# A second Strassen step for pairs of text units, and half of the adapter's turns on VectorE

## The chip, the cores and the metric

One core of a Trainium2 chip runs the whole program. The metric is the time of one execution in microseconds on the device (us below). TensorE (PE in the profile; its weight loads are PEld), VectorE (DVE), ScalarE (ACT), GpSimd (POOL) and SyncE (SP, which here only issues DMAs) each work through their own list of instructions in order, and wait for each other by semaphores.

## What is computed

The reference is a cross attention with an adapter path, all in float32. `x` is 2 batches of 2048 rows of 640 columns, `ctx` 2 batches of 128 tokens of 384 columns; the last 4 tokens are the adapter's.

```python
residual = x
enc, ca = ctx[:, :124], ctx[:, 124:]
query, keyt, valt = x @ Wq, enc @ Wk, enc @ Wv
hs = _mha(query, keyt, valt)                       # 8 heads of 80
ca_q1 = einsum('btc,th->bch', ca, Wq_ca)[:, indices, :]   # 2048 rows, indices = linspace(0, 383, 2048)
ca_hs1 = _mha(ca_q1, residual, residual)
ca_hs2 = _mha(ca_hs1 @ Wq, ca @ Wk_ca, ca @ Wv_ca)
out = (hs + ca_hs2) @ Wout + b_out + residual
```

Since `ca_q1` holds only 384 different rows for each batch, the adapter path is worked out for these 384, and its result (`o2`) is added to the output rows by an index at the end.

## The kernel before

**How the order is set.** Every operation of the program is issued by a `Desk` (line 66). Pieces of work are generators that yield `Do(engine, function, what it waits for, rooms it needs)`; `Desk.run` (line 351) issues them in the order of a table of whole numbers, `TURNS` (line 85 on), one number for each operation: the number divided by 6 is the place in the order, the remainder names the engine. So the table sets the program order of each engine and, where an operation may run on either of two engines, which one takes it. On the chip each engine keeps its program order and waits for semaphores alone; the table's numbers are no times.

**TensorE's helpers.** `matmul` (L396) is a plain product. `by_columns` (L405) splits a product with 128 output rows over the four column groups of 32 of the array, which work at the same time. A float32 product takes two passes, so a product of 128x128 by 128xN through `by_columns` is four rows in the order and 8 MATMUL records of width N in the trace. I call these 8 a **set** of width N. `transpose` (L410) turns a 128x128 block by a product with the identity (a turn, below). VectorE, ScalarE and GpSimd operations all pass through `call` (L427), DMAs through `dma` (L447).

**Stages.** At the start, weights and the first rows are loaded and turned, and small combined weights (`pk`, `pa`, `pyz`, `pv`) are made; VectorE spreads turned pieces and copies, and turns the rows of `x` with its own transposes (`xi` to `xt`, four instructions of 128x512 and one of 128x4x128 for each block of 512 rows). Then 8 blocks of queries follow (`pq`), mixed with the adapter's first pass over the scores (`s`, maxima `mx` by VectorE), and the text scores (`sc`, `softmax`), whose probabilities go to HBM and come back turned (`kept`, `pT`).

**The adapter** (`adapter(b)`, line 1869, for batch b = 0, 1): after the maxima, `spread` leaves them in `mt`, two halves j of 128x384 (j = 0, 1). For each half TensorE turns three blocks of 128x128 (`pm`), VectorE adds them to `ca`, and both halves are split into `cop` together. Then comes the second pass over the scores with `cop`, in 12 pieces for each half, whose exponentials are contracted with the values (`contract`, line 1985, tile `acc`). At the end of each half TensorE turns three blocks of `accs` into `pt_acc`, and after both halves `second(b)` (line 2030) makes `o2`.

**The text units.** 16 units m of 256 rows (two tiles of 128 rows each) go through `probabilities(m)` (line 2242) and `text_out_fast(m)` (line 2392). This takes the heads' outputs `ph` into `hs` (four chunks of 128 and a fifth that is apart), makes the sums s1 to s4 of a Strassen step (on VectorE or GpSimd), and takes (256 rows x 512) by (512 x 640) in seven products of half size rather than eight: 7 products of two chunks each, and four products for the fifth chunk, so 18 sets of width 320 (`HALF`). They stand in four chains of 4, 2, 1 and 1 steps (`chains`); a chain accumulates in one PSUM bank `po`, and after each step VectorE adds what the bank holds by then into a quarter (128 rows x 320 columns) of the residual rows (`add` in `chain`). A step waits for the add of the step before it in its chain. The residual rows lie in two times four row slots (`x_more`, `last_rows`), a tile each; when a tile has its sums, `stored` lets GpSimd add `o2` by an indirect DMA (L2351) and sends it out. The last unit had `o2` added earlier, and its halves of 320 columns go out one by one (`stored_half`).

## Time and profile before

| what | value |
|---|---|
| time, median of 3 runs | 573.14 us (573.0 to 573.99) |
| the profiled execution, its own time | 573.35 us |
| its span in the profile | 571.3 us |
| granted TensorE clock | 1.00 throughout |
| busy share of the span | PE 99%, PEld 54%, DVE 69%, ACT 50%, POOL 28% |
| MATMUL records | 8069 |

The span runs from the first to the last record of the profiled execution. The time of the same execution is 2.05 us longer, and it stands 0.21 us above the median. Times in rows are in us unless ns is said; a row of groups gives busy time and the mean of one instruction, then the idle time of the engine ahead of it; a row of a timeline gives its start and its length, and joins instructions of one kind that follow each other.

### The profile page before, as it was taken

How to read it: one execution, taken by the hardware profiler on the slowest of the kernel's cores; microseconds unless marked ns; L12 is line 12 of the kernel's file. 1: busy time of each engine (PE TensorE's matmuls, PEld its weight loads, DVE VectorE, ACT ScalarE, POOL GpSimd, SP SyncE). 2: the span in 40 equal slices, each digit the busy share in tenths (PEclk: the TensorE clock that was granted, in tenths of full speed). 3: DMA queues.
4: the chain of work that ended last, by engine and by line, in shares of the span. 5: the costliest groups of instructions: out<-in, count | busy, mean ns of one | idle time of the engine just before them, and what ended most of it. 6: DMA issues, size and time to landing. Idle time of an engine off the chain costs nothing.

```text
span 571.3 us, 18875 instructions
## 1 busy us (share of the span) xinstructions
PE 563.6 (99%) x8069; PEld 310.0 (54%) x8069; DVE 394.4 (69%) x659; ACT 286.7 (50%) x806; POOL 159.8 (28%) x213
## 2 busy tenths in 40 slices
PE   9999999999999999999999999999999999999997
PEld 8885335455555455466554554554555554445553
DVE  4366999999998577458999999998332213544443
ACT  2021355645566899899876654524554664100000
POOL 9102041114440731100004350531203053045152
PEclk9999999999999999999999999999999999999999
DMA  8998576965968977446746969977476587799888
GB/s 246 211 248 126 139 161 157 172 179 139 211 212 153 215 182 211 146 126 198 233 158 203 316 180 319 245 217 230 96 263 120 164 206 223 248 211 213 258 156 237
DMA packets 145691, 113.21 MB, mean 198 GB/s; under 512 B 82548, under 2 KB 116980, under 8 KB 145608
## 3 DMA queue, kind: packets, MB, share of 16 engines
q1 hardware_dynamic: 137000, 95.10, 60.0%
q0 software_dynamic: 5632, 10.69, 11.7%
q10 hardware_dynamic: 2976, 6.23, 3.2%
q8 instruction: 63, 1.03, 0.8%
q14 instruction: 20, 0.16, 0.1%
HBM read 71.60 MB, written 40.39 MB: 196 GB/s over the span
## 4 chain that ended last, share of the span: by engine, by line
PE 92%; DVE 3%; ACT 3%; DMA 1%; issue 1%; SPq 0%; ACTq 0%; DVEq 0%
PE po L405 27%; PE pq L405 24%; PE sc L396 7%; PE acc L396 7%; PE s L396 7%; PE ph L396 6%; PE pq L396 4%; PE pyz L396 2%; ACT ea L427 2%; DVE mx L427 2%; PE pv L396 1%; PE pk L396 1%; DMA xz<-in_x_dram 1%; ACT p L427 1%; PE pt_wq L410 1%
## 5 line engine op out<-in xcount | busy, mean ns | idle before, releaser
L427 ACT ACTIVATE p<-sc,m 128x124 f32<-128x124 f32 x256 | 90.1, 381 | 43.4 <-DVE m L427 38.4
L427 DVE TENSOR_REDUCE mx<-s 128x4 f32<-128x2048 f32 x48 | 109.0, 2271 | 1.9 <-PE s L396 1.9
L427 ACT ACTIVATE ea<-s 128x2048 f32<-128x2048 f32 x48 | 90.5, 1884 | 31.4 <-PE s L396 30.9
L405 PE MATMUL po<-wout_sums,hs 128*32 128x320 f32 x1024 | 78.5, 434 | 0.1
L405 PE MATMUL po<-wout_sb,hs 128*32 128x320 f32 x928 | 72.4, 433 | 0.0
L427 POOL TENSOR_TENSOR p<-p,r 128x992 f32<-128x992 f32 x17 | 31.4, 1847 | 130.9 <-DVE r L427 130.9
L405 PE MATMUL pq<-xt,wq_sb 128*32 128x256 f32 (+1 forms) x928 | 66.4, 418 | 0.0
L427 DVE TENSOR_TENSOR last_rows<-last_rows,po 128x320 f32<-128x320 f32 x60 | 28.1, 480 | 44.0 <-PE po L405 43.9
L427 ACT ACTIVATION_READ_ACCUMULATOR p<-sc,m 128x1 f32 x256 | 57.0, 223 | 0.0
L427 DVE TENSOR_TENSOR x_more<-x_more,po 128x320 f32<-128x320 f32 x68 | 32.4, 481 | 34.5 <-PE po L405 32.5
L405 PEld LDWEIGHTS po<-wout_sums,hs 128*32 128x32 f32 x1024 | 33.4, 110 | 32.7 <-issue 2.8
L427 DVE TENSOR_REDUCE m<-sc 128x4 f32<-128x496 f32 x64 | 40.8, 663 | 14.1 <-PE sc L396 14.0
L396 PE MATMUL acc<-ea,y_sb 128*32 128x384 f32 (+2 forms) x768 | 50.2, 382 | 0.2 <-ACT ea L427 0.2
L396 PE MATMUL ph<-pT,vpad 128*32 128x256 f32 x768 | 47.9, 381 | 0.0
L405 PEld LDWEIGHTS po<-wout_sb,hs 128*32 128x32 f32 x928 | 30.1, 110 | 28.2 <-issue 1.6
L2351 POOL DMA_INDIRECT x_more<-o,query x17 | 26.6, 1563 | 67.0 <-DVE x_more L427 31.1
L405 PEld LDWEIGHTS pq<-xt,wq_sb 128*32 128x32 f32 x928 | 27.7, 110 | 28.0 <-issue 13.4
L427 ACT COPY hs<-ph 128x512 f32<-128x512 f32 (+1 forms) x25 | 13.4, 551 | 57.7 <-PE ph L396 57.7
L427 DVE STREAM_TRANSPOSE eb<-p 128x1024 f32<-128x1024 f32 x32 | 39.4, 1233 | 1.2 <-POOL p L427 1.1
L396 PEld LDWEIGHTS sc<-kmain,q 64*128 64x128 f32 x512 | 31.8, 187 | 12.6 <-issue 5.8
L427 POOL TENSOR_TENSOR hs<-hs 128x256 f32<-128x256 f32 x31 | 28.9, 1019 | 33.9 <-ACT hs L427 25.6
L396 PE MATMUL sc<-kmain,q 64*128 64x124 f32 x512 | 38.0, 285 | 0.0
(219 smaller groups left out, 835.0 us busy)
## 6 DMA issues: line engine op xcount, KB each, us to landing
kept<-eb SPq DMA_DIRECT2D x32, 512.0 KB
pT<-kept SPq DMA_DIRECT2D x16, 1024.0 KB
landing<-away SPq DMA_DIRECT2D x15, 512.0 KB
xi<-in_x_dram SPq DMA_DIRECT2D x56, 128.0 KB
x_more<-in_x_dram SPq DMA_DIRECT2D x17, 320.0 KB
last_rows<-in_x_dram SPq DMA_DIRECT2D x15, 320.0 KB
y<-yt SPq DMA_DIRECT2D x16, 256.0 KB
y_sb<-y SPq DMA_DIRECT2D x32, 128.0 KB
```

Of the source, the lines that this page charges most:

```text
L396: self.pin(self.nc.tensor.matmul(out, lhsT, rhs, **kw))
L405: self.pin(self.nc.tensor.matmul(out[j : j + 32], lhsT[:, j : j + 32], rhs, **kw))
L410: self.pin(self.nc.tensor.transpose(out, in_, ident))
L427: self.pin(getattr(engine, what)(*args, **kw))
L2351: desk.pin(nc.gpsimd.indirect_dma_start(out=t, out_offset=None, in_=o2_of[b], in_offset=bass.IndirectOffsetOnAxis(ap=query[:, st : st + 1] ...
```

## The change

**Text units.** Ten of the 16 units are joined in five pairs, `PAIRED = ((6, 7), (3, 12), (9, 14), (10, 11), (8, 15))`. Three of the seven products of a unit's Strassen step (p = 0, 1, 2) are no longer taken for each unit apart: `joint` takes each for the two units of a pair at once, by a second Strassen step inside (two units x two chunks by two chunks x two halves of 160 columns), seven products of 128x160 rather than eight. `take_inner` makes the weights' inner differences once (`inner_w`, and two freed tiles `p_0`, `p_1`; 12 subtractions), `joint` the inner sums of `hs` for each pair (`inner_x`, 8 operations). The products stand in chains of 4, 2, 1 and 1 steps of width 160 (`inner_chain`, tiles `pi_n_p_c`), and each step is added by VectorE to an eighth (128 x 160) of the residual rows. Of a paired unit's own chains there remain the first and a step that is added to two quarters. The units' order is now 0, 4, 2, 1, 5, 13 and then the pairs; `probabilities` of a paired unit waits until the unit before has its room. The last unit's step of one product is split in two parts of 160 columns, and its first tile goes out in quarters.

**The adapter.** Only half j = 0 of the maxima is turned by TensorE. Half j = 1 is turned by VectorE in 16 transposes of 32x3x32 (`turned_blocks`), in a piece of work of its own (`other_half`), and the second pass of j = 0 waits for its own half of `cop` only. Of the four `pt_acc`, that of batch 1, half 0, is turned by VectorE too.

**The start.** `load_ca` waits for the masks only, the clearing of `vpad` for `ctx`, and all of `TURNS` holds new numbers. In the program lists, SP's load of `w_k` now stands behind all four loads of `xi` of the second block, where it stood ahead of them.

**Counts in the order, before and after:** sets of width 320 in the text units 288 and 196; sets of width 160 there 0 and 169; turns for `pm` 12 and 6, for `pt_acc` 12 and 9; VectorE adds of 128x320 into the rows 128 and 106, of 128x160 0 and 124; inner sums of `hs` 0 and 40 (20 on VectorE, 20 on GpSimd), inner differences of the weights 0 and 12 (5 and 7); VectorE transposes of 32x3x32 0 and 48; sums of `x` on VectorE 7 and 2, on GpSimd 17 and 22.

In the lists below line numbers of after are its own: L425, L434, L439 and L456 are `matmul`, `by_columns`, `transpose` and `call`, which were L396, L405, L410 and L427.

TensorE towards the end of the adapter's second pass of batch 1, where units of the text stand between its pieces (`po_n` is chain n of a unit, `wout_sums` holds sums of the weights and also the fifth chunk of `hs`; x4 and x8 are one and two sets). Before, a piece in which two units' chains alternate:

```order
L405 MATMUL po_0_6335<-wout_sums,hs_5064 32x320 x8
L405 MATMUL po_2_6537<-wout_sb,hs_5064 32x320 x8
L405 MATMUL po_2_6537<-wout_sb,wout_sums 32x320 x4
L405 MATMUL po_2_6554<-wout_sb,hs_4229 32x320 x8
L405 MATMUL po_2_6554<-wout_sb,wout_sums 32x320 x4
L405 MATMUL po_0_6568<-wout_sb,hs_4229 32x320 x8
L405 MATMUL po_1_6398<-wout_sums,hs_5064 32x320 x8
L405 MATMUL po_1_6398<-wout_sb,wout_sums 32x320 x4
L405 MATMUL po_0_6335<-wout_sb,wout_sums 32x320 x4
L405 MATMUL po_0_6568<-wout_sums,hs_4229 32x320 x8
```

And after, the same stretch of the program (`pi_0_0_6444` is the chain of four steps of product p = 0 of one pair; `p_834` and `p_835` hold inner differences of the weights):

```order
L434 MATMUL pi_0_0_6444<-wout_sb,hs_4137 32x160 x4
L434 MATMUL pi_2_0_6349<-wout_sb,wout_sums 32x160 x4
L434 MATMUL pi_1_0_6458<-wout_sb,hs_4137 32x160 x4
L434 MATMUL pi_0_0_6444<-p_834,inner_x_5623 32x160 x4
L425 MATMUL acc_1_5909<-ea_1_10_6387,y_sb 32x256 x8
L434 MATMUL pi_0_0_6444<-p_834,inner_x_5623 32x160 x4
L425 MATMUL acc_1_5909<-ea_1_11_6441,y_sb 32x128 x4
L425 MATMUL acc_1_5909<-ea_1_11_6441,y_sb 32x384 x4
L434 MATMUL pi_0_0_6444<-wout_sb,wout_sums 32x160 x4
L434 MATMUL pi_1_0_6458<-p_835,inner_x_5624 32x160 x4
```

Steps of a chain of width 160 now stand between those of others: the first two of `pi_0_0_6444` have two sets of width 160 between them, where the two steps of `po_0_6568` before have four sets of width 320.

VectorE at the start, before (`k_160` from the loaded `w_k`, `k_414` from TensorE's `p_kca`, then the first transpose of the second block's rows):

```order
L427 COPY k_160<-w_k 128x3x4x16 x2
L427 COPY k_414<-p_kca 128x128
L427 COPY k_414<-p_kca 128x16 x2
L427 TENSOR_TENSOR wide<-k_414,quarter 128x128
L427 TENSOR_REDUCE own<-ident 128x4
L427 TENSOR_SCALAR own<-own,side_83 128x4 x2
L427 TENSOR_REDUCE fold<-ident 128x32
L427 STREAM_TRANSPOSE xt_1_395<-xi_1_275 128x512
```

And after, from the copy out of `p_kca` on (now `k_420`):

```order
L456 COPY k_420<-p_kca 128x128
L456 COPY k_420<-p_kca 128x16 x2
L456 STREAM_TRANSPOSE xt_1_378<-xi_1_285 128x512
L456 TENSOR_TENSOR wide<-k_420,quarter 128x128
L456 TENSOR_REDUCE own<-ident 128x4
L456 TENSOR_SCALAR own<-own,side_83 128x4 x2
L456 TENSOR_REDUCE fold<-ident 128x32
L456 STREAM_TRANSPOSE xt_1_378<-xi_1_285 128x512 x3
L456 COPY k_160<-w_k 128x3x4x16 x2
L456 STREAM_TRANSPOSE xt_1_378<-xi_1_285 128x4x128
```

The two copies of `w_k` into `k_160` have moved from ahead of the copy out of `p_kca` to behind four transposes of `xt_1`. On TensorE the product that reads them (`pk_482`) stands here after, with the first rows that follow:

```order
L439 MATMUL pt_k_467<-ident,k_420 128x128
L425 MATMUL pt_k_467<-fold,wide 128x6
L425 MATMUL unread<-zeros 128x128
L439 MATMUL pt_wqca<-ident,wqca_sb 128x4 x2
L439 MATMUL pt_wqca<-ident,wqca_rest 128x4 x3
L425 MATMUL pk_482<-ctxT,k_160 128x256 x3
L425 MATMUL pa_0_494<-first_rows,blk_k 32x128 x16
```

Before, that product (`pk_457`) stood three rows behind `p_kca`; it is now the last ahead of `pa`.

TensorE between the adapter's two passes of batch 1 (`pm` turns the maxima), before:

```order
L405 MATMUL po_0_5181<-wout_sums,hs_5064 32x320 x8
L410 MATMUL pm_0_5227<-ident,mt_5190 128x128 x3
L410 MATMUL pm_1_5234<-ident,mt_5190 128x128 x3
L405 MATMUL po_0_5197<-wout_sums,hs_4130 32x320 x8
L405 MATMUL po_0_5181<-wout_sums,hs_5064 32x320 x8
L405 MATMUL po_0_5197<-wout_sums,hs_4130 32x320 x8
```

And after:

```order
L434 MATMUL po_0_None<-wout_sb,hs_4225 32x320 x8
L439 MATMUL pm_5220<-ident,mt_5188 128x128 x3
L434 MATMUL po_0_None<-wout_sums,hs_5066 32x320 x8
L434 MATMUL po_0_None<-wout_sums,hs_4225 32x320 x8
L434 MATMUL po_0_None<-wout_sums,hs_5066 32x320 x8
```

Of two groups of three turns one is left.

The diff, cut to its core:

```diff
     TURNS = {
-        ".1": [995], ".2": [44, 59, 60, 84, 96, 108, 114, 120, 126, 132, 150, 174, 198, 210, 234, 978], ".3": [608],
...
+    def turned_blocks(to, t, after):
+        for i in range(4):
+            def turn(i=i):
+                for g in range(4):
+                    desk.v_transpose(to[G * g : G * (g + 1), :, i], t[G * i : G * (i + 1), :, g])
+            yield Do("DVE", turn, after if i == 0 else None, rank=0)
...
-            "POOL", lambda: [desk.g_memset(vpad[b], 0.0) for b in range(B)], [("x", 0, 0)], marks=["vpad"]
+            "POOL", lambda: [desk.g_memset(vpad[b], 0.0) for b in range(B)], ["ctx"], marks=["vpad"]
...
-        op = yield Do("POOL", lambda: load_ca(b), [("cop", b - 1)] if b else ["masks", ("x", 0, 0)])
+        op = yield Do("POOL", lambda: load_ca(b), [("cop", b - 1)] if b else ["masks"])
...
+        yield from halves_of(cop[:, 0], less[:, 0], "c", marks=[("cop", b, 0)], rank=0)
+        yield Fork(other_half(b, less, mt, at, spread_at), 0)
...
-                    pm = bank(s[0], f"pm_{b}_{j}")
...
-        yield from halves_of(cop, less, "c", frees=[(eas, at)], marks=[("cop", b)], rank=0)
...
-                op = yield Do("PE", scores, [("cop", b)], needs=[(quad, 1), (eas, 1)], mode=(32, P))
+                op = yield Do("PE", scores, [("cop", b, j)], needs=[(quad, 1), (eas, 1)], mode=(32, P))
...
+        if (b, j) == (1, 0):
+            frees = [(eas, i)]
+            yield from turned_blocks(
+                turned.rearrange("p (a g k) -> p a g k", a=NCC, g=4),
+                accs.rearrange("p (a i k) -> p a i k", a=NCC, i=4), None,
+            )
...
+        if m in pair_of_unit:
+            chains = (chains[0], (((s3, t3, None), [("hs", m, "s3")], ((1, 1), (1, 0))),))
...
+    def joint(n, pair):
...
+            steps_of = (
+                (([(a[0][0], w[0][0])], [], (0, 0)), ([(s2, t2)], x(1), (1, 0)), ([(s1, t1)], x(0), (0, 1)),
+                 ([fifth(1, 1)], ends_h, (1, 1))),
+                (([(s3, t3)], x(2), (1, 1)), ([(a[1][1], t4), fifth(1, 0)], ends_h, (1, 0))),
+                (([(a[0][1], w[1][0]), fifth(0, 0)], ends_h, (0, 0)),),
+                (([(s4, w[1][1]), fifth(0, 1)], x(3) + ends_h, (0, 1)),),
+            )
...
+    def inner_chain(n, pair, p, c, steps, ready, rank):
...
+            op = yield Do(
+                "PE", product, after + at + ready, needs=[(banks, 1)] if k == 0 else [], mode=(P, 32), rank=rank
+            )
...
+                t = xr_of[pair[r]][i][0][:, u * HALF + v * HALF // 2 : u * HALF + (v + 1) * HALF // 2]
+                desk.b_tensor_tensor(t, t, po[:, : HALF // 2], ALU.add)
```

229 lines of the change are left out of this document (182 added, 47 removed), and 440 rows, old and new, of the table TURNS.

## The prediction

> **What bounds the kernel now.** The page first: the span, the busy times, the chain that ended last, and the two dearest groups of the products that the change touches; behind them, from the groups of TensorE by shape, the fifth-chunk products.
>
> ```profile
> span 571.3 us, 18875 instructions
> PE 563.6 (99%) x8069; PEld 310.0 (54%) x8069; DVE 394.4 (69%) x659; ACT 286.7 (50%) x806; POOL 159.8 (28%) x213
> PE 92%; DVE 3%; ACT 3%; DMA 1%; issue 1%; SPq 0%; ACTq 0%; DVEq 0%
> L405 PE MATMUL po<-wout_sums,hs 128*32 128x320 f32 x1024 | 78.5, 434 | 0.1
> L405 PE MATMUL po<-wout_sb,hs 128*32 128x320 f32 x928 | 72.4, 433 | 0.0
> ```
> ```profile
> L405 PE MATMUL po<-wout_sb,wout_sums 128*32 128x320 f32 x352 | 31.2, 433 | 0.0
> ```
>
> The reader is to see that TensorE is busy for 99% and is 92% of the chain, with next to no idle time ahead of the products: time taken off TensorE is time off the span as long as no other engine becomes late. 1024 + 928 + 352 = 2304 records are 288 sets of 8. Who could become late is read from the windows of 20 us (columns: window, length, then busy time and count of PE, PEld, DVE, ACT and POOL, then granted clock, DMA share, GB/s).
>
> ```profile
> 60.00:80.00 20.00, 20.00 (x204) 6.72 (x200) 19.49 (x27) 7.91 (x26) 6.07 (x7) 1.00 0.62 154
> 120.00:140.00 20.00, 20.00 (x316) 10.50 (x312) 19.98 (x26) 11.03 (x43) 7.81 (x5) 1.00 0.53 140
> 440.00:460.00 20.00, 20.00 (x323) 10.33 (x319) 5.22 (x12) 12.24 (x9) 1.91 (x2) 1.00 0.66 194
> 540.00:560.00 20.00, 20.00 (x308) 11.84 (x304) 8.70 (x21) 0.37 (x1) 12.03 (x9) 1.00 0.86 187
> ```
>
> VectorE is full at 60 to 80 and 120 to 140, but has half the time or more to spare at 440 and at 540, and that is where the change puts its narrow adds.
>
> **Term 1, the products.** What does a set cost? Of width 320 from the tail, of width 160 from one small product at the start that has this very form.
>
> ```profile
> 562.62 3.44 PE L405 MATMUL po<-wout_sums,hs 128*32 128x320 f32 x48
> 565.85 1.29 PE L405 MATMUL po<-wout_sb,hs 128*32 128x320 f32 x16
> ```
> ```profile
> 52.82 1.00 PE L396 MATMUL pvca<-w_vca,caT 128*32 128x160 f32 x24
> 53.64 1.47 PE L405 MATMUL pq<-xt,wq_sb 128*32 128x512 f32 x12
> ```
> ```profile
> 52.82 0.67 PEld L396 LDWEIGHTS pvca<-w_vca,caT 128*32 128x32 f32 x20 [0.30 <-issue]
> ```
>
> From start to start, 48 records (six sets) took 565.85 − 562.62 = 3.23, so 0.538 a set of 320; 24 records (three sets) of width 160 took 53.64 − 52.82 = 0.82, so 0.273. Before: 288 x 0.538 = 154.9. After: 196 x 0.538 + 169 x 0.273 = 105.4 + 46.1 = 151.6. I take **−3.4** (the 92 wide sets that go are worth 184 narrow ones, and 169 come: 15 narrow sets, with a little off for a narrow set that is dearer than half a wide one). The bound below is 15 x 0.273 = −4.1. The bound above is the other product of this width, which went through between two of another form:
>
> ```profile
> 31.56 1.02 PE L396 MATMUL p_kca<-w_kca,cadT 128*32 128x160 f32 x24
> 32.51 0.33 PE L410 MATMUL pt_wq<-ident,wq 128*128 128x128 f32 x1
> ```
>
> 0.95 for three sets is 0.317 each: 169 x (0.317 − 0.273) = 7.4 more, so +4.0. It holds the change of form at both ends, which the new sets, mostly among their like, seldom have; so I stay with 0.273. The loads speak for that too, though closely: 0.67/20 = 33.5 ns a load, so 8 in 0.268 beside products of 0.273.
>
> The Trainium skill, "TensorE: Matmul & The Clock Gate", section "Back-to-back issue gap", speaks against narrow products: it says that a sustained stream of loads and products goes at about 81 ns each at width 128, where the product alone would allow 56. As an estimate from that page, a ratio of 81/56 on 0.273 would make 0.39 a set and add about 20 us. The 24 records of `pvca` took 34 ns each with four column groups at work, so this trace does not agree for so short a stream; no row shows a long one.
>
> **Term 2, the turns.** Two groups of three `pm` and one of three `pt_acc` go from TensorE.
>
> ```profile
> 442.39 0.55 PE L410 MATMUL pt_acc<-ident,accs 128*128 128x128 f32 x3
> 442.87 0.51 PE L396 MATMUL s<-cop,zop 32*128 32x384 f32 x8
> ```
>
> A group took 442.87 − 442.39 = 0.48: 3 x 0.48 = **−1.4** (0 if TensorE then waits for VectorE instead). The 48 small transposes come to VectorE ahead of the second pass or at a half's end, where other products stand ready and VectorE, by the window at 440, works 5 of 20 us. If that cover is gone, half j = 1 is late by its 16 transposes; half j = 0 goes first with its own half of `cop`, so it does not wait for them.
>
> **Term 3, the start.** The order shows VectorE's copies of `w_k` behind four transposes, and `pk` right ahead of `pa` on TensorE. How late is `pk` then?
>
> ```profile
> 30.57 0.84 DVE L427 COPY k<-w_k 128x192 f32<-128x192 f32 x2
> 32.65 0.45 DVE L427 COPY k<-p_kca 128x128 f32<-128x128 f32 x3 [1.23 <-PE p_kca L396]
> 34.31 0.70 DVE L427 STREAM_TRANSPOSE xt<-xi 128x512 f32<-128x512 f32 x1
> 36.51 1.29 DVE L427 STREAM_TRANSPOSE xt<-xi 128x512 f32<-128x512 f32 x2
> 37.73 0.35 DVE L427 TENSOR_SCALAR blk_k<-pt_k,side 128x24 f32<-128x24 f32 x2
> 38.00 0.26 DVE L427 TENSOR_TENSOR blk_k<-pt_k,own 128x24 f32<-128x24 f32 x2
> ```
> ```profile
> 24.70 0.28 PE L410 MATMUL pt_wqca<-ident,wqca_sb 4*128 4x4 f32 x2
> 25.10 0.65 PE L410 MATMUL pt_wq<-ident,wq_sb 128*128 128x128 f32 x4
> ...
> 32.68 1.46 PE L396 MATMUL pq<-xt,wq 128*128 128x256 f32 x6
> 33.97 1.46 PE L396 MATMUL pk<-ctxT,k 128*128 128x256 f32 x6
> 35.27 0.60 PE L410 MATMUL pt_wq<-ident,wq_sb 128*128 128x128 f32 x4
> 35.71 0.27 PE L410 MATMUL pt_wq<-ident,wq 128*128 128x128 f32 x1
> 35.81 1.03 PE L396 MATMUL pq<-xt,wq 128*128 128x256 f32 x4
> 36.68 0.27 PE L410 MATMUL pt_k<-ident,k 128*128 128x128 f32 x1
> 36.93 1.54 PE L396 MATMUL pk<-ctxT,w_k 128*128 128x256 f32 x6
> 38.40 1.08 PE L396 MATMUL pa<-first_rows,blk_k 128*32 128x128 f32 x32
> ```
>
> Counted from the end of `p_kca` (32.51 before): VectorE starts 0.14 later, needs 34.31 − 32.65 = 1.66 for the copies, `wide`, `own` and `fold`, then (37.73 − 36.51)/2 = 0.61 for each of four transposes, so 2.44, then 0.84 for the copies of `w_k`: 5.1; and TensorE starts 0.14 after VectorE is done (38.00 + 0.26 = 38.26, then `pa` at 38.40): 5.2. TensorE has in the meantime `pq` x4 twice (0.87, from 35.81 to 36.68), two single turns and the filler `unread` (0.10 each, from 35.71 to 35.81), four turns (0.44), `pq` x6 (1.29), `pt_k` (0.25) and the small turns of `wqca` (25.10 − 24.70 = 0.40): 4.4. So `pk` waits about **+0.8**, and nothing covers it, since `pa` and all behind it stand in line on TensorE. The bounds are 0 and +2.5: SP now loads `w_k` behind the four loads of `xi`; if it lands after VectorE gets to it, all that is behind it is later too, and the four transposes (2.44) are my measure of by how much.
>
> **Term 4, waits of the narrow chains.** A step waits for the add of the step before.
>
> ```profile
> 561.00 1.82 PE L405 MATMUL po<-wout_sb,hs 128*32 128x320 f32 x24
> 561.27 0.49 DVE L427 TENSOR_TENSOR x_more<-x_more,po 128x320 f32<-128x320 f32 x1 [0.59 <-PE po L405]
> ```
> ```profile
> 542.11 1.28 DVE L427 TENSOR_TENSOR last_rows<-last_rows,po 128x320 f32<-128x320 f32 x3 [1.74 <-PE po L405]
> ```
> ```profile
> 33.14 0.29 DVE L427 TENSOR_TENSOR wide<-k,quarter 128x128 f32<-128x128 f32 x1
> ```
>
> The add starts 0.27 behind the next product's start (561.00 to 561.27), a wide one lasts 0.49, one of 128 columns 0.29, so a narrow one about 0.32; with the 0.14 back to TensorE a narrow step needs 0.73 from the one before it, a wide one 0.90. Among the `pi` in the order four steps have only two narrow sets, 0.55, in between (as the first two of `pi_0_0_6444` in the rows shown), and two `po` have three, 0.82; the rest have more. 4 x 0.18 + 2 x 0.08 = 0.9 if VectorE is free at each; with some adds that queue behind each other I take **+1.0**. The bound below is 0. Above it is +5: the 30 chains of `pi` with several steps have 60 steps that wait for one before, and a third of these would wait 0.25.
>
> Other edits go at **0**. Five sums of `x` leave VectorE for GpSimd where VectorE is full; if they hold TensorE up now, it gains, but the rows of the window at 60 show TensorE busy for all of 20.00, so I count nothing, and −1 as the bound. The 40 inner sums and the 12 differences lie under products of other units and cost a wait only with the third rival below. The last add is narrower by 0.17, against more and smaller stores behind it.
>
> **The sum** is made on the profiled execution: 571.3 − 3.4 − 1.4 + 0.8 + 1.0 = 568.3. What lies around the span was 573.35 − 571.3 = 2.05, so 570.35 there; that execution is 0.21 above the median, so **570.1**.
>
> **The rivals.**
>
> *A long stream of narrow sets is paced by its weight loads, not by its products.* At 0.317 a set, the row of `p_kca`, 570.1 + 7.4 = 577.5; at 0.29 it is 573. For it, the loads fill 0.268 of 0.273 already; against it, `pvca`, in which three sets in a row held 0.273. This is the mechanism that the page of the Trainium skill speaks of; by its own figures the time would be some 590.
>
> *VectorE becomes the bound in the pairs* (the case of the other side). From the last unit's `ph` to the end TensorE has 13 wide and 37 narrow sets and six sets of 256 for `ph`, 0.43 each by width: 7.0 + 10.1 + 2.6 = 19.7. VectorE has 9 wide and 28 narrow adds, 3 copies and 8 sums there. By pitch a wide add takes (1.28 − 0.48)/2 = 0.40 and a narrow one 0.17 less, 0.23; with each copy and sum at a wide add's 0.40 that is 3.6 + 6.4 + 4.4 = 14.4, and TensorE leads. If a narrow add costs what a wide one does alone, 0.49, since each waits for its own product, it is 37 x 0.49 + 4.4 = 22.5, 2.8 more than TensorE; it decides from (19.7 − 3.6 − 4.4)/28 = 0.42 a narrow add. The pairs before have other work on VectorE beside (softmax, `second`); with 2.8 for each of three pairs, 8.4 in place of my 1.0: 577.5, slower.
>
> *More comes off*: no wait at the start, none in the chains, the full 4.1 and 1 from the sums of `x`: 571.3 − 4.1 − 1.4 − 1.0 + 2.05 − 0.21 = 566.6.
>
> *It does not do what it says*: TensorE has 4.8 less to do and waits as much elsewhere, at the start (+2.5) and for rooms of `inner_x`, of which there are two for five pairs: 573.1.
>
> **How the numbers follow.** Forecast 570.1, its own range 568.5 to 571.9: 0.56. More off, 566.6: 0.10. The gain eaten by waits, or narrow sets at 0.29, near 573: 0.14. Narrow sets at 0.317: 0.08. VectorE as the bound: 0.12. A measurement can tell 0.2% from no change, so faster is below 572.0 and slower above 574.3: 0.66, 0.14, 0.20. For 8 in 10 the range reaches from 567.0 to 575.5.
>
> **What would show it.** A narrow set's spacing in the tail near 0.27; PE's busy time about 4.8 lower; the first `pa` after a wait of 0.8 put down to VectorE's `k`; idle time ahead of `pi` of about 1 in all. I would be wrong if idle time of TensorE ahead of `pi` and `po` is above 4, if VectorE's window at the end is above 17 of 20, or if the spacing of narrow sets is above 0.29.

## The result, and the profile after

The changed kernel took 577.68 us (median of 5 runs, 575.72 to 578.93) against 573.14 for the kernel before: a ratio of **1.0068, with a 95% interval of 1.0055 to 1.0081**. The ratio is taken over the single runs of both kernels, not from the two medians, whose quotient, 1.0079, lies inside the interval. It is 0.7% slower, where 570.1 was forecast and 575.5 was the end of the range. Its profiled execution took 575.96, with a span of 574.3; that is 1.7 below its median, so the profile below shows 3.0 of the 4.5 us.

The page of the changed kernel: the span, the busy times and the chain that ended last.

```profile
span 574.3 us, 20322 instructions
PE 562.4 (98%) x8676; PEld 328.1 (57%) x8676; DVE 438.4 (76%) x831; ACT 284.9 (50%) x804; POOL 181.4 (32%) x242
PE 88%; DVE 4%; ACT 4%; DMA 1%; POOL 1%; issue 1%; DVEq 0%; SPq 0%; ACTq 0%
```

TensorE's busy time fell by 1.2 only, and its share of the chain from 92% to 88%; a record's busy time also covers time that it spends beside the next one (a narrow set has 0.45 or more in the rows below, and the next can start 0.27 after it), so the work itself has to be read from start to start. The chain of waits of the changed kernel has two long stretches of nothing but narrow products (start, length, count):

```profile
518.04 3.53 PE pi L434 x104
...
538.36 3.53 PE pi L434 x104
```

3.53/104 is 34 ns a record, **0.272 for a set of 8**, as forecast. If each form of product is given its usual spacing, the changed kernel's products need 3.5 us less than those of before and its turns 1.1 less: 4.6 in all. What passes beyond that spacing I call TensorE's loss. It is no larger than before up to 180 us, 2.5 larger from 180 to 480, and from 480 to the last product it is **6.2 instead of 2.4**. Its last product starts at 568.5 (566.7 before), and 5.8 us pass from there to the end of the span (4.6 before). −4.6 + 2.5 + 3.8 + 1.2 makes 2.9 of the 3.0.

So the pairs (behind 480 us) are where to look. First the windows of before that were not shown yet, then those of the changed kernel (length; busy time and count of PE, PEld, DVE, ACT, POOL; clock; DMA share; GB/s).

```profile
480.00:500.00 20.00, 19.84 (x303) 9.71 (x299) 9.67 (x25) 5.21 (x8) 5.25 (x4) 1.00 0.72 203
500.00:520.00 20.00, 20.00 (x316) 10.06 (x312) 8.45 (x20) 1.17 (x2) 8.40 (x8) 1.00 0.92 210
520.00:540.00 20.00, 20.00 (x322) 10.55 (x315) 9.37 (x23) 1.17 (x2) 6.15 (x5) 1.00 0.87 232
```
```profile
480.00:500.00 20.00, 19.15 (x363) 12.09 (x363) 11.19 (x35) 4.98 (x7) 3.47 (x3) 1.00 0.68 201
500.00:520.00 20.00, 19.60 (x412) 12.86 (x408) 14.97 (x42) 0.59 (x1) 10.50 (x10) 1.00 0.94 252
520.00:540.00 20.00, 19.61 (x416) 14.40 (x412) 15.39 (x43) 1.45 (x3) 7.94 (x8) 1.00 0.77 192
540.00:560.00 20.00, 20.00 (x432) 13.43 (x428) 14.93 (x47) 0.00 (x0) 13.96 (x12) 1.00 1.03 248
```

VectorE goes from 8 to 10 of 20 to 11 and 15 of 20, never above the 17 that the prediction had set as its alarm, and behind 500 ScalarE has next to nothing to do. What VectorE does from 480 to 568 is seen in its groups (busy us, mean ns, then its idle time ahead and what ended that), of before first:

```profile
L427 DVE TENSOR_TENSOR x_more<-x_more,po 128x320 f32<-128x320 f32 x29 | 14.0, 485 | 13.5 <-PE po L405 13.3
L427 DVE TENSOR_TENSOR last_rows<-last_rows,po 128x320 f32<-128x320 f32 x28 | 13.1, 484 | 20.1 <-PE po L405 20.0
```
```profile
L456 DVE TENSOR_TENSOR last_rows<-last_rows,pi 128x160 f32<-128x160 f32 x47 | 13.9, 316 | 4.8 <-PE pi L434 4.8
L456 DVE TENSOR_TENSOR x_more<-x_more,pi 128x160 f32<-128x160 f32 x41 | 12.3, 317 | 6.8 <-PE pi L434 6.4
L456 DVE TENSOR_TENSOR x_more<-x_more,po_None 128x320 f32<-128x320 f32 x22 | 10.5, 484 | 6.1 <-PE po_None L434 6.0
L456 DVE TENSOR_TENSOR last_rows<-last_rows,po_None 128x320 f32<-128x320 f32 x18 | 8.5, 483 | 3.6 <-PE po_None L434 3.5
L456 DVE COPY hs<-ph 128x512 f32<-128x512 f32 (+1 forms) x8 | 4.9, 618 | 3.3 <-PE ph L425 3.3
```

57 wide adds, 27.1 us, have become 40 wide and 88 narrow ones, 45.2 us: a narrow add costs 0.316, two thirds of a wide one. In before VectorE is idle for 33.6 us ahead of its adds, nearly all of it for products; now for 21.3. So it still has time to spare, and yet TensorE now waits for it. The list of TensorE's waits behind 480 in the changed kernel (total, times, longest), where before had one of 0.2 only:

```profile
PE pi L434 <- DVE x_more L456: 0.7, 2, 0.4
PE po L425 <- DVE o L456: 0.5, 1, 0.5
PE pi L434 <- POOL inner_x L456: 0.3, 1, 0.3
```

The list names 1.5 us, less than half of the 3.8 that were lost more: it counts from a record's modelled end, and leaves out short waits. Two of these places, in the changed kernel's timeline:

```profile
504.79 0.48 DVE L456 TENSOR_TENSOR x_more<-x_more,po_None 128x320 f32<-128x320 f32 x1
504.88 0.45 PE L434 MATMUL pi<-wout_sb,wout_sums 128*32 128x160 f32 x8
505.36 0.32 DVE L456 TENSOR_TENSOR x_more<-x_more,pi 128x160 f32<-128x160 f32 x1
505.60 0.88 DVE L456 TENSOR_TENSOR x_more<-x_more,po_None 128x320 f32<-128x320 f32 x2
505.73 0.48 PE L434 MATMUL pi<-inner_w,hs 128*32 128x160 f32 x8 [0.40 <-DVE x_more L456]
```

A narrow set starts at 504.88 and could be followed 0.27 later; the next needs the bank of an add that VectorE comes to only at 505.36, behind inner sums and a wide add that started at 504.79. The set starts at 505.73: 0.58 lost, of which the row shows 0.40, since a record's end is modelled later than the next one could start.

```profile
492.81 0.69 ACT L456 COPY o<-po 128x640 f32<-128x640 f32 x1 [1.76 <-PE po L425]
...
493.53 0.82 DVE L456 COPY o<-po 128x640 f32<-128x640 f32 x1 [1.34 <-ACT o L456]
...
494.27 0.31 DVE L456 TENSOR_TENSOR last_rows<-last_rows,pi 128x160 f32<-128x160 f32 x1
...
494.41 0.81 PE L425 MATMUL po<-w_sb,p2T 32*128 32x320 f32 x4 [0.51 <-DVE o L456]
```

Here VectorE stands idle for 1.34 us, at a copy that starts only when ScalarE's copy out of the same tile `po` has ended, with an add of the pairs queued behind it until 494.27. An engine that is busy for half of a window can hold others up for as long as it stands at one instruction.

### The profile page after: what moved, and what is told of

Same layout as the page of the kernel before. It is cut to its first block, busy times and chain, and to the rows that moved or that the text cites. A ratio compares the mean times of both kernels' runs of the same rounds, so it can differ in the third digit from the quotient of the medians.

```text
span 574.3 us, 20322 instructions
## 1 busy us (share of the span) xinstructions
PE 562.4 (98%) x8676; PEld 328.1 (57%) x8676; DVE 438.4 (76%) x831; ACT 284.9 (50%) x804; POOL 181.4 (32%) x242
## 4 chain that ended last, share of the span: by engine, by line
PE 88%; DVE 4%; ACT 4%; DMA 1%; POOL 1%; issue 1%; DVEq 0%; SPq 0%; ACTq 0%
PE pq L434 22%; PE po_None L434 18%; PE pi L434 8%; PE sc L425 7%; PE acc L425 7%; PE s L425 6%; PE ph L425 6%; PE pq L425 4%; PE pyz L425 3%; DVE mx L456 1%; ACT p L456 1%; ACT ea L456 1%; PE pv L425 1%; PE pk L425 1%; DMA landing<-away 1%; PE unread L425 1%
## 5 line engine op out<-in xcount | busy, mean ns | idle before, releaser
L456 ACT ACTIVATE p<-sc,m 128x124 f32<-128x124 f32 x256 | 90.2, 377 | 52.4 <-DVE m L456 49.6
L456 DVE TENSOR_REDUCE mx<-s 128x4 f32<-128x2048 f32 x48 | 109.2, 2275 | 1.9 <-PE s L425 1.6
L456 ACT ACTIVATE ea<-s 128x2048 f32<-128x2048 f32 x48 | 90.7, 1889 | 37.8 <-PE s L425 33.7
L456 POOL TENSOR_TENSOR p<-p,r 128x992 f32<-128x992 f32 x19 | 35.8, 1882 | 133.3 <-DVE r L456 133.3
L434 PE MATMUL pq<-xt,wq_sb 128*32 128x256 f32 (+1 forms) x928 | 66.6, 418 | 0.0
L434 PE MATMUL po_None<-wout_sums,hs 128*32 128x320 f32 x848 | 66.0, 434 | 0.1
L456 ACT ACTIVATION_READ_ACCUMULATOR p<-sc,m 128x1 f32 x256 | 55.9, 219 | 0.0
L425 PE MATMUL acc<-ea,y_sb 128*32 128x384 f32 (+2 forms) x768 | 50.8, 382 | 0.2 <-ACT ea L456 0.2
L456 DVE TENSOR_REDUCE m<-sc 128x4 f32<-128x496 f32 x64 | 40.5, 663 | 10.4 <-PE sc L425 10.3
L425 PE MATMUL ph<-pT,vpad 128*32 128x256 f32 x768 | 48.1, 380 | 0.0
L2408 POOL DMA_INDIRECT x_more<-o,query x17 | 27.1, 1595 | 62.1 <-DVE x_more L456 32.6
L434 PE MATMUL po_None<-wout_sb,hs 128*32 128x320 f32 x568 | 44.9, 434 | 0.4 <-ACT hs L456 0.4
L434 PEld LDWEIGHTS pq<-xt,wq_sb 128*32 128x32 f32 x928 | 27.7, 109 | 27.6 <-issue 13.5
L434 PEld LDWEIGHTS po_None<-wout_sums,hs 128*32 128x32 f32 x848 | 26.5, 110 | 24.5 <-issue 1.9
L456 DVE STREAM_TRANSPOSE eb<-p 128x1024 f32<-128x1024 f32 x32 | 39.3, 1230 | 0.9 <-POOL p L456 0.4
L2408 POOL DMA_INDIRECT last_rows<-o,query x15 | 24.3, 1618 | 49.4 <-DVE last_rows L456 41.4
L425 PEld LDWEIGHTS sc<-kmain,q 64*128 64x128 f32 x512 | 32.0, 187 | 12.9 <-issue 3.9
L425 PE MATMUL sc<-kmain,q 64*128 64x124 f32 x512 | 38.3, 285 | 0.8 <-ACT p L456 0.8
L456 POOL TENSOR_TENSOR hs<-hs 128x256 f32<-128x256 f32 x28 | 24.6, 931 | 36.8 <-ACT hs L456 22.5
L425 PEld LDWEIGHTS ph<-pT,vpad 128*32 128x32 f32 x768 | 25.0, 110 | 17.9 <-issue 2.9
L456 DVE TENSOR_TENSOR x_more<-x_more,po_None 128x320 f32<-128x320 f32 x58 | 27.2, 480 | 9.9 <-PE po_None L434 9.4
L434 PE MATMUL pq<-xt,wq 128*32 128x512 f32 x280 | 34.1, 595 | 0.0
```

What stands on the lines that cost most here:

```text
L425: self.pin(self.nc.tensor.matmul(out, lhsT, rhs, **kw))
L434: self.pin(self.nc.tensor.matmul(out[j : j + 32], lhsT[:, j : j + 32], rhs, **kw))
L456: self.pin(getattr(engine, what)(*args, **kw))
L2408: desk.pin(nc.gpsimd.indirect_dma_start(out=t, out_offset=None, in_=o2_of[b], in_offset=bass.IndirectOffsetOnAxis(ap=query[:, st : st + 1] ...
```

## The experiments

**Theory A**: the products got cheaper as forecast, and TensorE now waits for VectorE, whose queue in the pairs (narrow adds, inner sums, copies of `hs` out of PSUM, the adapter's last steps) is late in bursts. Its rivals were that the new order of the work makes TensorE wait whatever VectorE's load, that the stores behind the last adds set the end, and that the turns given to VectorE cost what they save. Each ratio is against the kernel before on the same chip; the changed kernel's is 1.0068 (1.0055 to 1.0081). The changed kernel itself was timed once, in five runs, and not again beside its variants, so they are compared with it by their ratios.

### small_adds: the narrow adds on 16 of 160 columns

```
-                desk.b_tensor_tensor(t, t, po[:, : HALF // 2], ALU.add)
+                desk.b_tensor_tensor(t[:, :16], t[:, :16], po[:, :16], ALU.add)
```

> The changed kernel with each of the 124 narrow adds of VectorE cut from 160 to 16 columns (the output rows are incomplete): 0.32 us becomes about 0.18, TensorE's work is untouched. Theory A, VectorE is late in the pair stage and TensorE's next step of a chain waits for it (some 3.6 us of TensorE's time between 480 and 560 us): 2 to 3 us faster than the changed kernel, so 575 to 576 us, and the gaps ahead of pi gone. Theory B, the loss lies at the end, in a store behind the last add: no change, 577 to 578. Theory C, it lies ahead of 480 us, in waits that the new order of all stages brings (ScalarE waiting for a DMA, adapter copies): no change, 577 to 578.

574.67 us (12 runs), ratio 1.0032 (1.0014 to 1.005). The groups of VectorE behind 480 in this kernel:

```profile
L456 DVE TENSOR_TENSOR last_rows<-last_rows,pi 128x16 f32<-128x16 f32 x46 | 6.7, 166 | 7.0 <-PE pi L434 6.6
L456 DVE TENSOR_TENSOR x_more<-x_more,pi 128x16 f32<-128x16 f32 x43 | 6.6, 168 | 9.3 <-PE pi L434 8.8
```

89 adds at 0.167 instead of 0.316 take 13 us of VectorE's time away, and the kernel is 0.36% faster by the ratios, 2.1 us; TensorE's loss behind 480 falls from 6.2 to 4.3, and no wait ahead of `pi` is left in its list. VectorE's time in the pairs is worth something.

### small_sums: the inner sums on 8 or 16 columns

```
+            desk.g_memset(ends, 0.0)
+            desk.g_memset(middle, 0.0)
...
-                    (desk.g_tensor_tensor if desk.engine == "POOL" else desk.v_tensor_tensor)(to[:, i], x, y, op_of)
+                    (desk.g_tensor_tensor if desk.engine == "POOL" else desk.v_tensor_tensor)(to[:, i][..., :8], x[..., :8], y[..., :8], op_of)
```

> The changed kernel with the 40 inner sums of hs cut from 256 or 128 columns to 8 or 16 (wrong products of the same size; two clearing writes more on GpSimd, once). Theory A in the form that the sums with two operands in SBUF are what makes VectorE and GpSimd late (they took 1.14 instead of 0.42 us beside a sum on GpSimd): 1.5 to 2.5 us faster, 575 to 576. Theory A in the form that the number of adds does it: under 1 us faster. Theories B and C: no change, 577 to 578.

575.4 us (6 runs), ratio 1.0032 (1.0019 to 1.0046): by the ratios, as much as the adds. But its profiled run, at 576.64 the longest of the six, shows a loss behind 480 of 6.9, no less than the 6.2 of the changed kernel. Where the gain lies was not seen.

### small_both, and before_small as its control

`small_both` makes both edits. `before_small` cuts the wide adds of the kernel before in the same way.

> The changed kernel with the narrow adds at 16 columns and the inner sums at 8 or 16, both (wrong output, TensorE's work untouched). If VectorE and GpSimd are the whole of what the pairs lose, TensorE's loss behind 480 us falls from 6.2 to about 2.4 as before the change, and the time by 3.5 to 4.5 us, to 573 to 574; if the adapter's second products, the end and the earlier stages hold a part that no VectorE work explains, it stays within 1 us of the kernel with small adds, 574 to 575.

574.07 us (12 runs), ratio 1.0024 (1.0007 to 1.004). Its trace, of a run of 574.39, has a loss behind 480 of 5.5: far from the 2.4 that the expectation gave if VectorE and GpSimd were the whole of it.

```
-                    desk.b_tensor_tensor(t, t, po[:, :HALF], ALU.add)
+                    desk.b_tensor_tensor(t[:, :16], t[:, :16], po[:, :16], ALU.add)
```

> Control: the kernel before, with its 128 wide adds cut from 320 to 16 columns (output incomplete). Its TensorE waits for no add in the trace, so the same time, 572.5 to 573.2; only the last add and store could give 0.3 us. If it is over 1 us faster, the gain of small adds in the changed kernel does not speak of the change.

572.75 us (12 runs), ratio 0.999 (0.9977 to 1.0002). What is worth 0.4% in the changed kernel is worth at most a little in the kernel before (0.1%, with 1 inside the interval). But even with hardly any adds and sums the changed kernel is not faster than before: there is more than their duration. Of the 5.5, 0.9 is a wait ahead of the last unit's `ph`, which comes back under `o_copy`.

### store_first: a whole store ahead of two of an eighth

One step of the last unit is moved, so that the small stores come last.

```
+    TURNS['.64.3.9'][2] = 15232
```

> The changed kernel with one store moved: the store of a whole tile of unit 8, which stands last on SyncE, behind the last eighth of the last unit, goes ahead of two eighths. Theory B (the end is set by that store, 0.43 us after the last eighth's and longer in flight): 0.7 to 1.2 us faster, 576.5 to 577. Theories A and C: no change; if the store's own data are late, the eighths behind it wait and it is up to 1 us slower.

575.94 us (7 runs), ratio 1.0047 (1.003 to 1.0065). In its profile 6.1 us lie between the last product and the end (5.8 in the changed kernel). So which of these stores comes last does not set the tail. That the stores as a whole hold the end up is not ruled out by this run, and its interval overlaps the changed kernel's.

### pe_turns: TensorE makes the turns of half j = 1 again

The small transposes of half j = 1 go from VectorE, three turns of `pm` in each batch come back to TensorE, and the table gets numbers for them. The core of the edit:

```
-        yield from turned_blocks(
-            less[:, 1].rearrange("p (a i k) -> p a i k", a=NCC, i=4),
-            mt[:, :, 1].rearrange("p a (g k) -> p a g k", g=4), [spread_at],
-        )
...
+        def turn_more(pm=op.value):
+            for ct in range(NCC):
+                transpose(pm[:, ct * P : (ct + 1) * P], mt[:, ct, 1, :], ident)
+
+        yield Do("PE", turn_more)
```

> The changed kernel with the maxima of half 1 turned by TensorE again in both batches (three turns and one add from PSUM each, in place of 16 transposes of VectorE; the half after batch 1's first stays with VectorE). If VectorE's transposes cost nothing, as predicted: 0.7 to 1.0 us slower, 578.5. Rival: the transposes delay what VectorE has next and TensorE waits for it: 0.5 to 1.5 us faster, 576 to 577.

577.62 us (6 runs), ratio 1.008 (1.0058 to 1.0101). Undoing this part gains nothing that these runs can tell: VectorE's turns are not what costs, within 0.2% or so.

### mended and mended_pairs: the waiting steps later

Where TensorE waited, its step was put some steps further back. `mended_pairs` does so at six places behind 480 us; `mended` at the same six, and at two ahead of 300 us, the first two lines, of which one moves a cast of ScalarE. (The expectation speaks of nine; there are eight.)

```
+    TURNS['.34.8.8'][3] = 5437
+    TURNS['.55.4'][3] = 7596
+    TURNS['.80.13'][6] = 12846
+    TURNS['.55.1.1.4'][8] = 13002
+    TURNS['.81.18'][2] = 13302
+    TURNS['.82.17'][2] = 14214
+    TURNS['.83.9'][4] = 15024
+    TURNS['.82.20'][0] = 14118
```

> The changed kernel with nothing but the places of nine operations in the lists altered: seven TensorE steps that wait in the trace of the changed kernel (pi steps at 488.3, 505.7, 531.3, 534.6 and 560.4 us, the adapter's second products at 494.4, its turns at 289.0) go one to four operations later, and ScalarE's copy of rests that waits for a DMA at 206.9 goes behind the exponentials that TensorE waits for. Theory A2, the loss is TensorE standing behind single late operations, where other products were ready: these waits (1.2, 0.6, 0.5, 0.7, 0.6, 0.7, 0.3, 0.1: 4.7 in all) go in good part, 2.5 to 4.5 us faster than the changed kernel, 573 to 575. Rival, VectorE is the bound over the pairs as a whole: the waits turn up at the next step, at most 1.5 us faster.

> The same for the six TensorE steps behind 480 us alone. Theory A2: 1.5 to 2.5 us faster than the changed kernel, 575 to 576; what the kernel of all nine gains beyond this is the share of the waits ahead of 300 us. Rival, VectorE as the bound of the pairs: under 0.7 us faster, and all that the other one gains lies ahead of 300 us.

`mended`: 575.74 us (6 runs), ratio 1.0048 (1.0034 to 1.0062). `mended_pairs`: 577.32 us (10 runs), ratio 1.0078 (1.0052 to 1.0105). Behind 480 nothing was gained: the loss there is 7.1 and 8.3 in their traces. In `mended_pairs` the waits are at other steps:

```profile
495.04 0.82 DVE L463 COPY o<-po 128x640 f32<-128x640 f32 x1 [1.32 <-ACT o L463]
...
495.78 0.31 DVE L463 TENSOR_TENSOR last_rows<-last_rows,pi 128x160 f32<-128x160 f32 x1
...
496.14 0.48 PE L441 MATMUL pi<-p,hs 128*32 128x160 f32 x8 [0.74 <-DVE last_rows L463]
```

VectorE's copy still stands idle for 1.3 us; now a step of the pairs, instead of the adapter's, waits behind it. So here it is VectorE's queue that is late, not one step of TensorE that stands too early. The two moves ahead of 300 us may be worth the rest of `mended` (the two ratios overlap). One of them is this place of the changed kernel, where ScalarE's cast waits for a DMA with four exponentials behind it that TensorE needs:

```profile
206.89 0.62 ACT L456 CAST rests<-landing 128x512 fp32r<-128x512 f32 x1 [1.23 <-DMA landing<-away]
...
208.95 0.94 PE L425 MATMUL sc<-kmain,q 64*128 64x124 f32 x12 [0.78 <-ACT p L456]
```

### copies_act: fifteen copies by ScalarE instead of VectorE

Nothing is taken out and no other operation moves; the copies of `hs` out of PSUM in the pairs change their engine, by a number that is one lower. Three of the fifteen lines:

```
+    TURNS['.68.3.2'][0] = 12055
+    TURNS['.68.3.1'][0] = 12103
...
+    TURNS['.71.3.3'][0] = 14689
```

> The changed kernel, but fifteen copies of the pairs' hs out of PSUM, which VectorE makes behind 480 us, are made by ScalarE, which is busy for 0 to 1.5 of 20 us there. Nothing is left out and the numbers of no other operation move. Theory A (VectorE falls behind as a whole in the pairs, and TensorE waits for its adds and inner sums): some 6 us less work on VectorE behind 480, so the waits there fall by 1 to 2 us: 575.7 to 576.7, ratio to the kernel before 1.0045 to 1.0062. Rival D (VectorE's load as such does not matter; the new order alone makes TensorE wait at places that are wrong): no change, 577.0 to 578.4, ratio 1.0067 to 1.009.

574.88 us (12 runs), ratio **1.003 (1.0013 to 1.0047)**: by the ratios 2.2 us less than the changed kernel, a little more than theory A had asked for, and rival D falls. Two windows of it:

```profile
520.00:540.00 20.00, 19.90 (x436) 15.19 (x432) 13.31 (x39) 2.99 (x6) 8.03 (x9) 1.00 0.85 216
540.00:560.00 20.00, 20.00 (x424) 13.20 (x420) 13.76 (x44) 1.54 (x3) 13.08 (x12) 1.00 1.01 225
```

From 15.39 to 13.31, and from 14.93 to 13.76 of 20: so little less on VectorE, and TensorE's loss behind 480 falls from 6.2 to 4.9. Yet it is not the places shown above that went. TensorE's waits behind 480 in this kernel:

```profile
PE pi L450 <- DVE x_more L472: 0.9, 2, 0.6
PE po L441 <- DVE o L472: 0.5, 1, 0.5
```

The wait for the copy of `o` is as long as before the relief, and the one at 505.73 (now 504.83) has grown from 0.40 to 0.61. What has gone from the list is the wait for GpSimd's inner sum; the rest of the gain is in waits too short for the list, and in other stages. Whether the adds come sooner or the copied `hs` itself does, these runs do not separate.

### before_copies: the same relief for the kernel before

> The kernel before (not the changed one), with its last eleven copies of hs out of PSUM moved from VectorE to ScalarE in the same way as copies_act does it. Nothing is left out. Theory A (only the changed kernel is short of VectorE in the pairs): within 0.15% of the kernel before, 572.3 to 574.0. Rival E (a less busy VectorE is worth 2 us whatever the kernel, so that copies_act tells nothing of the change): 570.8 to 571.8, ratio 0.996 to 0.9977.

572.39 us (12 runs), ratio 0.9998 (0.9985 to 1.0011). In before VectorE has the time, and relieving it is worth nothing that can be told (0.1% either way): rival E falls. What `copies_act` won back is the change's doing.

### front_copies and relieved

`front_copies` is `copies_act` with the two moves ahead of 300 us; `relieved` has the six moves behind 480 as well.

> As copies_act, and the two moves ahead of 300 us that mended had (ScalarE's cast of a weight four exponentials later; the first turn of the second half of the adapter somewhat later). Nothing is left out. Theory A with the part ahead of 300 us: those two moves are worth the 1.6 us that lay between mended and mended_pairs, so 574.1 to 575.1, ratio 1.002 to 1.0035. Rival D: as mended, 575.4 to 576.0, ratio 1.004 to 1.005.

> As front_copies, and with the six TensorE steps behind 480 us put behind the VectorE or GpSimd operation that they waited for (mended's). Nothing is left out. Theory A: with VectorE relieved and the steps in a better order, 573.3 to 574.6, ratio 1.0005 to 1.0026, near the kernel before. Rival D: the moves behind 480 did nothing by themselves (mended_pairs), so as front_copies within 0.5 us.

`front_copies`: 574.19 us (12 runs), ratio 1.002 (1.0007 to 1.0034). `relieved`: 575.46 us (12 runs), ratio 1.0038 (1.0023 to 1.0054). The two moves ahead of 300 us may gain some tenths (the interval overlaps that of `copies_act`); the six behind 480 gain nothing, once more.

### o_copy: the adapter's last copy by ScalarE too

`front_copies`, and the copy at 493.53 above:

```
+    TURNS['.55.1.1.4.3'][0] = 12949
```

> As front_copies, and the copy of the adapter's last products out of PSUM that VectorE makes at 493.5 us, after an idle time of 1.3 us with adds queued behind it, is made by ScalarE. Nothing is left out. Theory A with the head of the queue counted: 0.5 to 0.8 us less than front_copies, 573.4 to 573.8, ratio 1.0005 to 1.0012. Rival F (the adapter's second products wait for the copy on whichever engine it is made): as front_copies within 0.3 us, ratio 1.0015 to 1.0025.

573.66 us (12 runs), ratio **1.0006 (0.9994 to 1.0018)**: equal to before within the measurement, and 0.62% (3.6 us) below the changed kernel, with only engines and numbers altered. What the last copy alone is worth is not settled: the interval overlaps that of `front_copies`, and rival F's range. The place in its timeline:

```profile
491.27 1.29 ACT L475 COPY o<-po 128x640 f32<-128x640 f32 x2 [1.76 <-PE po L444]
...
492.43 0.49 DVE L475 TENSOR_TENSOR last_rows<-last_rows,po_None 128x320 f32<-128x320 f32 x1 [1.55 <-PE po_None L453]
492.61 0.81 PE L444 MATMUL po<-w_sb,p2T 32*128 32x320 f32 x4 [0.25 <-ACT o L475]
```

Both copies end after 1.29 us on ScalarE; TensorE waits 0.25 instead of 0.51, and VectorE waits for a product, with nothing late behind it. But the loss is not gone. In its profiled run (574.34, above its median) TensorE loses 6.5 behind 480, where before lost 2.4. The largest part that can be named stands in its waits and in its chain (start, length):

```profile
PE ph L444 <- DMA pT<-kept: 1.4, 1, 1.4
```
```profile
537.15 10.48 DMA pT<-kept
```

A load of 1 MB for the last unit needed 10.48 us among the stores, and TensorE waited 1.4 for it. The profiles of before and of the changed kernel show no such wait, but other variants do, `small_sums` for one:

```profile
PE ph L425 <- DMA pT<-kept: 0.5, 1, 0.5
```

In `small_adds` it is 0.2. In `small_both` the list puts the 0.9 ahead of the same product down to an add of VectorE's, but the load landed at 546.93 and the product started at 547.06, 0.13 later, as it did behind the landing in the other three. The load's issue and the first product that reads it, before and after:

```profile
524.66 0.40 SPq L447 DMA_DIRECT2D pT<-kept  x1
537.42 1.94 PE L396 MATMUL ph<-pT,vpad 128*32 128x256 f32 x32
```
```profile
540.35 0.42 SPq L476 DMA_DIRECT2D pT<-kept  x1
548.45 2.77 PE L425 MATMUL ph<-pT,vpad 128*32 128x256 f32 x48
```

From issue to use there were 12.8 us before, and there are 8.1 now, where loads of this tile took from 7.5 to 10.5 in the variants. In the changed kernel SyncE sends it behind loads and stores of rows that wait in its list, so hardly any time is left until TensorE has to wait for it. No run sends it earlier, and what it costs the timed runs is open. Without it `o_copy` still loses 5.0 behind 480: it equals before because its products and turns are 4.6 cheaper.

### copies_all: eight more copies by ScalarE, between 400 and 480 us

> As o_copy, and the eight copies of hs that VectorE makes between about 400 and 480 us are made by ScalarE too, which also makes the exponentials there. Nothing is left out. Theory A taken further back: 0.5 to 1.5 us less than o_copy, 572.2 to 573.3, ratio 0.9985 to 1.0005. Rival G (ahead of 480 us the exponentials, and not VectorE, set what TensorE waits for): as o_copy or up to 1 us more, ratio 1.0005 to 1.003.

575.03 us (12 runs), ratio 1.0039 (1.0021 to 1.0057): 1.4 us slower than `o_copy` on the same chip. As rival G had it, if with more than its 1 us, ScalarE is not the place for VectorE's work here, where it also makes the exponentials; that these are the reason is argued, not shown. The waits of TensorE that the trace of this kernel lists between 400 and 480, of 0.9 and 0.8, stand ahead of products of the output, put down to no engine; `o_copy` has one of 0.3 there.

No version of the changed kernel that was run beats the kernel before. The best, `o_copy`, equals it.

## Why the prediction was wrong

**What bounds the kernel** was read rightly: TensorE does, and time off it counts as long as no other engine is late. The condition failed.

**Term 1, the products (−3.4)** was right: −3.5 by spacing, at 0.272 a narrow set against 0.273 taken, and the rival of load-paced sets (0.29 to 0.317) falls. The rule of the Trainium skill ("TensorE: Matmul & The Clock Gate", section "Back-to-back issue gap"), by which a long stream would be slower than products of this width alone, is not borne out by the stretches of 104 records at 34 ns.

**Term 2, the turns (−1.4)**: −1.1 by spacing. By the times this part can't be told from nothing (`pe_turns` 1.008 against 1.0068).

**Term 3, the start (+0.8)**: the wait is there, but shorter. VectorE's copies of `w_k` end 0.14 ahead of `pk`, in the changed kernel:

```profile
35.48 0.80 DVE L456 COPY k<-w_k 128x192 f32<-128x192 f32 x2
```
```profile
36.42 1.53 PE L425 MATMUL pk<-ctxT,k 128*128 128x256 f32 x6
```

The loss up to 60 us is 0.2 larger than before, and by 180 us nothing is left of it, though the prediction had nothing to cover it.

**Term 4, the waits of the narrow chains (+1.0, at most +5)**, is one of the two steps that failed. It took VectorE to be free at each add, "with some adds that queue behind each other"; what TensorE lost more behind 480 us came to +3.8 in the profiled run, the adapter's wait for VectorE's copy included. The prediction had every number for VectorE's load: it had worked out that 0.42 a narrow add decides, and measured here one lasts 0.316, so on average VectorE keeps up, as the windows at 15 of 20 say. What it left out is that the adds stand in one queue with copies, sums and the adapter's steps, some of which last or wait 0.8 to 1.3 us, while TensorE makes a narrow set every 0.27 and soon needs a bank back. `copies_act` with its control `before_copies` shows that VectorE's load there costs time, and that it does so in the changed kernel only: 2.2 us by the ratios, of 3.9 that this kernel is slower. They do not show that the queue is the whole of the 3.8. With hardly any adds and sums (`small_both`) 3.1 more than before are still lost there, and in `o_copy` 2.6, the wait for the load left out.

The sign of being wrong that the prediction named for this would not have gone off: the trace's list has 1.0 of idle time ahead of `pi`, the very figure forecast, and 0.9 ahead of `po`, not above 4. The loss shows only from start to start.

**The other edits at 0** are the other step that failed. Inner sums are part of the load (`small_sums`, 0.4%). 2.5 us were lost between 180 and 480 in the profile, where ScalarE's and VectorE's orders moved; of that only the places at 207 and 289 were tried, with an uncertain gain. The end is 1.2 later behind the last product. In the windows the DMA engines have a share of 1.03 from 540 to 560, against 0.86 before, and the last store goes out at 569.81, 0.46 behind the end of the last add; that the stores make the end longer is not shown.

**The sum of it.** The span was forecast as 568.3 and measured as 574.3. Of the 6.0 between them, term 4 has 2.8, the stretch from 180 to 480 has 2.5 and the end 1.2, where nothing was counted; term 2 has 0.3, and term 3 gives back 0.8. The bound of +5 on term 4 held. What carried the time out of the range were the parts put at nothing, and what the profile does not hold.

**The rivals**: "VectorE becomes the bound in the pairs" named the engine and, at 577.5, nearly the time; but its mechanism (a rate: 0.49 a narrow add in the last unit, 2.8 a pair) is not what happened, and that its time comes so near is luck. It got 0.12. The alarm "above 17 of 20" would not have gone off either.

**What stays open**: the profiles show 3.0 of the 4.5 us, and the rest is in no trace; how the 2.5 us between 180 and 480 divide; what the late load of the last unit costs; and what, beside VectorE's load, makes up the loss behind 480.

## What to carry to other kernels

Halving the width of a product halved TensorE's time for it here, but not the time of the add behind it (0.316 against 0.484 us) and not the number of things that stand in that add's queue: count the instructions of the engine that gives banks back, and ask how long its longest wait is, not how full its window is. Here moving single steps of TensorE only moved the wait, while giving some of the late engine's work to one that is idle in that stage won 2.2 us back. Check such a gain on the kernel before as well, so that it is known to belong to the change, and read the loss from start to start: the list of waits named less than half of it. And look at the loads that a new order sends later than before: here one of them was the next thing to be waited for.

## What the runs showed of the hardware

In these traces VectorE's sums of two operands in SBUF are longer when GpSimd makes such a sum at the same time. The tile `hs` on VectorE behind 480 us, before and after (shortest/median/longest ns), and one place of the changed kernel:

```profile
L427 DVE TENSOR_TENSOR hs<-hs x17: 415/419/426, 481.8 to 548.1; 128x256 f32<-128x256 f32 x17
```
```profile
L456 DVE TENSOR_TENSOR hs<-hs x16: 407/419/1140, 489.6 to 554.2; 128x256 f32<-128x256 f32 x16
```
```profile
529.56 1.14 DVE L456 TENSOR_TENSOR hs<-hs 128x256 f32<-128x256 f32 x1
529.69 1.57 POOL L456 TENSOR_TENSOR inner_x<-hs,inner_x 128x256 f32<-128x256 f32 x1
531.32 0.48 PE L434 MATMUL pi<-wout_sums,inner_x 128*32 128x160 f32 x8 [0.26 <-POOL inner_x L456]
```

A sum of 0.42 takes 1.14 beside a sum on GpSimd that itself takes 1.57, and TensorE's next product waits for the latter. In the whole trace of the changed kernel seven sums of this width into `hs` and `inner_x` on VectorE lie beside a `TENSOR_TENSOR` of GpSimd, and six of them take 0.52 to 1.14; the other 43 take 0.41 to 0.43. For GpSimd the sign is weaker: its sums of this width take about 0.73 or 1.3 with no such sum of VectorE beside them, and 1.57 or 1.58 only with one.

The Trainium skill, "SBUF — State Buffer", section "Who interferes with whom", states that a VectorE instruction with two SBUF inputs contends with a GpSimd instruction that reads SBUF. The trace agrees. It agrees too where the Trainium skill says in that section that a VectorE instruction with at most one SBUF input, outside the two-port modes, does not contend with GpSimd: the adds with an operand in PSUM had 0.48 and 0.32 throughout behind 480.

So inner sums that are split between the two engines can slow each other, which no duration taken from a stage with one of them at work shows.
